# Graph attention, four layers on one core: the adjacency mask turned by DMA engines in place of the tensor engine

## The chip, the cores and the metric

One core of a Trainium2 chip runs the kernel. The metric is the device time of one execution in microseconds (us); a lower one is better. The kernel before took 3196.11 us, the median of 3 runs (3195.84 to 3197.12).

## The reference: what is computed

16 graphs of 1024 nodes with 256 features pass through four layers of graph attention. Each layer normalises the features, cuts them at zero, projects them with a 256 x 256 matrix, and lets each node take a weighted mean over its neighbours. The weights of a row come from one number of the row's node and one of the neighbour, and are zero where the adjacency is zero.

```python
# one layer, cut to what matters; adj is (16, 1024, 1024) int32, here 0 or 1
h  = relu(layernorm(x))
Wh = h @ W
e  = leaky_relu((Wh @ a1)[:, :, None] + (Wh @ a2)[:, None, :])
e  = where(adj == 0, -1e9, e)
x  = x + softmax(e, -1) @ Wh
```

Layers 1 and 2 have another activation and an ELU behind the sum; layer 3 has four heads of 64 features, a bias, a ReLU with the projection added, and a normalisation per head.

## The kernel before, in words

**Tiling.** A graph is called a batch `b`. Its 1024 nodes lie as 8 blocks of 128 on the 128 partitions (`NI = 8`, `P = 128`). `x_b` holds the features, `mask` the adjacency turned over, one byte for each pair: partition and block name the neighbour `j`, the free position names the node `i`. `mask` and `x_b` have three buffers each.

**Loading (`load`, L96 to L124).** `load(b)` is a generator that gives control back at each `yield`. It issues the DMA of the features on the SP queue (L99), and for each block of 128 rows a DMA on the POOL queue that reads int32 and writes bf16 (L106, two ahead, three buffers). For each block, ScalarE sums the squares of adjacency minus a half into `squares` (L117; this later checks that every entry is 0 or 1), TensorE turns the eight 128 x 128 squares of the block into PSUM (L122, tile `misc`), and ScalarE copies them as bytes into `mask` (L123).

**A layer (`attend`, L352).** `weigh` (L268) lays one number of each node along the free axis (L276, on TensorE), and VectorE makes the weights of one neighbour block: maximum or minimum of two terms, times the mask (L280). TensorE multiplies the weights with the projected features (`product`, L367; L471 for the heads of layer 3). `finish` adds the result to `x_b` (L296 to L307, the last addition on POOL), and `project` (L233) makes the projection of the next layer, whose statistics need VectorE and a power on POOL (L227), whose transposes and products run on TensorE (L252, L259), and whose evictions run on ScalarE (L254, L320, L322, L341).

**Order of the work.** Two streams, the even and the odd batches, are traced in turns by hand-written costs (`yield 0.9` and so on), the second `LAG = 120` behind the first; so one stream's last layer lies beside the other's middle layers. The framework then orders each engine's instructions by this priority and by when it takes their inputs to be ready; each engine works through its own queue in that order. `batch(b)` makes `coming = load(b + 2)` and advances it once after each of the eight half-heads of layer 3 (L482), and to its end after the last (L498). `stream(1)` runs `load(1)` ahead of its first batch (L511). `load(0)` and `prepare()`, which fetches and extends the weights, are begun before the streams (L516) and finished behind the first projection (L415), before the first `attend`.

**Output.** After layer 3, POOL does the last scaling and addition (`rescale`, L445, L446), and two DMAs on the SP queue write the batch (L502).

Of the kernel before, what the change touches and what calls it, by code (L numbers as in the profile page):

```python
# [32 lines left out]
F32 = mybir.dt.float32  # L33
BF = mybir.dt.bfloat16
U8 = mybir.dt.uint8
I16 = mybir.dt.int16
I32 = mybir.dt.int32
AF = mybir.ActivationFunctionType
ALU = mybir.AluOpType
AX = mybir.AxisListType  # L40

P = 128
# [17 lines left out]
def short_path(ctx: ExitStack, tc: tile.TileContext, ins: dict, out: bass.AP, bad: bass.AP):  # L60

    nc = tc.nc
    x, adj = ins["x"], ins["adj"]
    B, N, D = x.shape
    H, T, E = ins["L3_a_src"].shape
    NI = N // P
    NK = D // P
    HALF = 512
    NH = N // HALF
    NG = HALF // P  # L70
    EXT = [3, 3, 3, 3 * H]
    AHEAD = 2
    LAG = 120.0

    const = ctx.enter_context(tc.tile_pool(name="const", bufs=1))
    nodes = ctx.enter_context(tc.tile_pool(name="nodes", bufs=3))
    adjs = ctx.enter_context(tc.tile_pool(name="adjs", bufs=3))
    wide = ctx.enter_context(tc.tile_pool(name="wide", bufs=2))
    psum = ctx.enter_context(tc.tile_pool(name="psum", bufs=2, space=bass.MemoryType.PSUM))

    ident = const.tile([P, P], F32, name="ident")
    make_identity(nc, ident)
    ident_b = const.tile([P, P], BF, name="ident_b")
    nc.vector.tensor_copy(ident_b, ident)
    minus_half = const.tile([P, 1], F32, name="minus_half")
    nc.vector.memset(minus_half, -0.5)
    ones = const.tile([P, P], F32, name="ones")
# [2 lines left out]
    squares = const.tile([P, B, NI], F32, name="squares")  # L90
    inverses = const.tile([P, B, NI], F32, name="inverses")


    xs, masks = {}, {}

    def load(b: int):  # L96

        xs[b] = nodes.tile([P, NI, D], F32, name="x_b")
        nc.sync.dma_start(xs[b], x[b].rearrange("(i p) f -> p i f", p=P))  # L99
        mask = masks[b] = nodes.tile([P, NI, N], U8, name="mask")  # L100
        fetched = {}

        def fetch(i: int):

            fetched[i] = adjs.tile([P, N], BF, name="adj_i")
            nc.gpsimd.dma_start(fetched[i], adj[b, ts(i, P), :])  # L106

        for i in range(AHEAD):
            fetch(i)
        yield  # L110
        for i in range(NI):
            if i + AHEAD < NI:
                fetch(i + AHEAD)
            adj_i = fetched.pop(i)

            every = wide.tile([P, N], BF, name="wide")
            nc.scalar.activation(  # L117
                every, adj_i, AF.Square, bias=minus_half, accum_out=squares[:, b, i : i + 1]
            )
            turned = psum.tile([P, NI, P], BF, name="misc")  # L120
            for j in range(NI):
                nc.tensor.transpose(turned[:, j, :], adj_i[:, ts(j, P)], ident_b)  # L122
            nc.scalar.copy(mask[:, :, ts(i, P)], turned)  # L123
            yield  # L124

    edges = ctx.enter_context(tc.tile_pool(name="edges", bufs=NI))
# [8 lines left out]
    bias = const.tile([P, D], F32, name="bias")  # L135
# [132 lines left out]
    def weigh(b: int, column, c, op, into: list):  # L268


        while row_taken:
            yield 0.25
        row_taken.append(b)
        r = psum.tile([P, N], F32, name="row", bufs=1)
        for i in range(NI):
            nc.tensor.transpose(r[:, ts(i, P)], column(i).to_broadcast([P, P]), ident)  # L276
        yield 0.5
        for j in range(NI):
            w = edges.tile([P, N], F32, name=f"weights{b % 2}")
            nc.vector.scalar_tensor_tensor(w, r, c(j), masks[b][:, j, :], op0=op, op1=ALU.mult)  # L280
            into.append(w)
            if j == NI - 1:
                row_taken.pop()
            yield 0.5
# [24 lines left out]
    def batch(b: int):  # L309
        xb = xs.pop(b)  # L310
        if b == 0:
            next(preparing)
        coming = load(b + 2) if b + 2 < B else iter(())

        def begin(l: int):

            V = nodes.tile([P, NI, H, E + 1], F32, name="V", bufs=4).rearrange("p i h e -> p i (h e)")

            def evict(i: int, projected: bass.AP, rstd: bass.AP):
                nc.scalar.activation(V[:, i, D : D + 3], projected[:, D:], AF.Exp, scale=rstd)  # L320
                if l == 2:
                    nc.scalar.mul(V[:, i, :D], projected[:, :D], rstd)  # L322
                else:
                    nc.vector.tensor_scalar(  # L324
                        V[:, i, :D], projected[:, :D], rstd, V[:, i, D : D + 1],
                        op0=ALU.mult, op1=ALU.mult,
                    )

            return V, evict

# [3 lines left out]
        def begin3():  # L334
            h3 = last["h3"] = single.tile([P, NI, D], F32, name="h3")
            V3 = nodes.tile([P, NI, H, E + 1], F32, name="V", bufs=4)
            ex = last["ex"] = small.tile([P, NI, 3 * H], F32, name="ex", bufs=2)

            def evict3(i: int, projected: bass.AP, rstd: bass.AP):
# [3 lines left out]
                nc.gpsimd.tensor_mul(  # L343
                    V3[:, i, :, :E], h3[:, i, :].rearrange("p (h e) -> p h e", h=H),
                    q.to_broadcast([P, H, E]),
                )
                nc.gpsimd.tensor_copy(V3[:, i, :, E:], q)
                nc.gpsimd.tensor_add(xb[:, i, :], xb[:, i, :], beta)

            return V3, evict3  # L350

        def attend(l: int, V: bass.AP, finish, then: int):  # L352

            weights = []
            behind = weigh(
                b, lambda i: V[:, i, D + 2 : D + 3], lambda j: V[:, j, D + 1 : D + 2],
                ALU.min if l == 1 else ALU.max, weights,
            )
            yield from start(behind, b)
            following = begin(then) if then < 3 else begin3()  # L360
            steps = iter(())
            accs = {}

            def product(i: int, j: int):
                if j == 0:
                    accs[i] = accumulator(b)[:, : D + 1]
                nc.tensor.matmul(  # L367
                    accs[i], weights[j][:, ts(i, P)], V[:, j, : D + 1],
                    start=(j == 0), stop=(j == NI - 1),
                )  # L370


            for j in range(NI):
                next(behind)
                product(0, j)
                product(1, j)
                yield 0.9
            for _ in behind:
                pass
            for i in range(NI):  # L380
                if i > 1:
                    for j in range(NI):
                        product(i, j)
                acc = accs.pop(i)
                finish(i, acc)
                if i != 0:
                    yield 3.6
                if i % 2 == 1:

                    yield from steps  # L390
                    steps = project(b, then, xb, i // 2, following[1])
                yield from islice(steps, 1)
            yield 1.0
            yield from steps
            return following[0]
# [16 lines left out]
        for steps in pairs:  # L412
            yield from steps
        if b == 0:
            for _ in chain(loading, preparing):  # L415
                pass
        V = yield from attend(0, V, finish0, 1)
        V = yield from attend(1, V, finish, 2)
        V3 = yield from attend(2, V, finish, 3)


        h3, ex = last["h3"], last["ex"]
        y = single.tile([P, NI, H, E], F32, name="y")
        normed = []
        shape = [P, NI, E]

        def center(h: int):

            yh = y[:, :, h, :]
            head = ts(h, E)  # L430
            nc.gpsimd.tensor_add(yh, yh, bias[:, head].unsqueeze(1).to_broadcast(shape))  # L431
            nc.vector.scalar_tensor_tensor(yh, yh, 0.0, h3[:, :, head], op0=ALU.max, op1=ALU.add)
            mean = small.tile([P, NI], F32, name="mean")
            nc.vector.tensor_reduce(mean, yh, AX.X, ALU.add)
            nc.vector.tensor_scalar_mul(mean, mean, 1.0 / E)
            nc.vector.tensor_sub(yh, yh, mean.unsqueeze(2).to_broadcast(shape))
            square = wide.tile(shape, F32, name="wide")
            nc.scalar.activation(square, yh, AF.Square)
            var = small.tile([P, NI], F32, name="var")
            nc.vector.tensor_reduce(var, square, AX.X, ALU.add)  # L440
            return yh, head, inverse_root(var, NI, L3_EPS, 1.0 / E)
# [18 lines left out]
        for n in range(H * NH):  # L460
            h, g = divmod(n, NH)
# [37 lines left out]
            pass  # L499
        rescale(*normed.pop())  # L500
        for g in range(NH):
            nc.sync.dma_start(  # L502
                out[b, ts(g, HALF), :].rearrange("(i p) f -> p i f", p=P),
                y[:, ts(g, NG)].rearrange("p i h e -> p i (h e)"),
            )
        yield 1.0

# [6 lines left out]
            yield from batch(b)  # L514

    loading, preparing = load(0), prepare()  # L516
    next(loading)
    next(preparing)
    streams = [[0.0, stream(0)], [LAG, stream(1)]]
    while streams:  # L520
        ahead = min(streams, key=lambda s: s[0])
        t = next(ahead[1], None)
# [381 lines left out]
```

## Time and profile before

| What | Value |
|---|---|
| Median of 3 runs | 3196.11 us |
| The profiled execution's own time | 3197.01 us |
| Its span in the profile | 3195.3 us |
| TensorE's mean granted clock | 0.991 |
| ScalarE, busy | 855.3 us (27%) |
| L123, mask eviction on ScalarE | 128 x, mean 1011 ns |
| L117, squares on ScalarE | 128 x, mean 1142 ns |
| L106, adjacency DMA, its issue on POOL | 128 x, mean 605 ns; 3.8 us to landing |
| L99, feature DMA | 16 x 1024 KB, 7.6 us to landing |
| L502, output DMA | 32 x 512 KB, 3.9 us to landing |

The profile gives, for each engine, the time in which it was busy, and for each group of instructions its count, its mean duration, and the idle time of the engine just before it with what ended that. "PE" is TensorE's matmul, "PEld" its weight load, which overlaps it; "DVE" is VectorE, "ACT" ScalarE, "POOL" GpSimd. Matmuls are pipelined: the mean duration of one is longer than the distance from one to the next, so what one costs in a dense row is read from starts in the timeline and not from its duration. The windows view gives busy time for each stretch of time; the timeline lists instructions of one engine with the idle time before them in brackets.

### The profile page before, as it was taken

How to read it: one execution, taken by the hardware profiler on the slowest of the kernel's cores; microseconds unless marked ns; L12 is line 12 of the kernel's file. 1: busy time of each engine (PE TensorE's matmuls, PEld its weight loads, DVE VectorE, ACT ScalarE, POOL GpSimd, SP SyncE). 2: the span in 40 equal slices, each digit the busy share in tenths (PEclk: the TensorE clock that was granted, in tenths of full speed). 3: DMA queues.
4: the chain of work that ended last, by engine and by line, in shares of the span. 5: the costliest groups of instructions: out<-in, count | busy, mean ns of one | idle time of the engine just before them, and what ended most of it. 6: DMA issues, size and time to landing. Idle time of an engine off the chain costs nothing.

```text
span 3195.3 us, 37581 instructions
## 1 busy us (share of the span) xinstructions
PE 3058.6 (96%) x13702; PEld 2112.1 (66%) x13702; DVE 2370.9 (74%) x5244; ACT 855.3 (27%) x1857; POOL 1002.4 (31%) x1286
## 2 busy tenths in 40 slices
PE   7899999999999999999999999999999999999987
PEld 5666776667666686666867667676676767766552
DVE  5576778777787767787687876878768787677756
ACT  3322223222232312323123231232313222232120
POOL 1223324232242322423224232342323323233332
PEclk8999999999999999999999999999999999999998
DMA  4101101111010100101001010111101111000000
GB/s 107 24 7 17 34 4 21 34 20 30 7 37 18 28 19 11 44 11 43 1 14 40 14 40 1 17 37 17 37 1 20 34 17 37 4 14 14 1 14 14
DMA packets 55951, 72.09 MB, mean 23 GB/s; under 512 B 5072, under 2 KB 38992, under 8 KB 55760
## 3 DMA queue, kind: packets, MB, share of 16 engines
q0 software_dynamic: 18432, 33.56, 6.9%
q1 hardware_dynamic: 37328, 36.05, 3.5%
q8 instruction: 111, 1.82, 0.2%
q14 instruction: 80, 0.66, 0.1%
HBM read 86.38 MB, written 16.78 MB: 32 GB/s over the span
## 4 chain that ended last, share of the span: by engine, by line
PE 71%; DVE 17%; POOL 6%; ACT 2%; issue 2%; DMA 1%; ACTq 0%; POOLq 0%; SPq 0%; DVEq 0%
PE acc L367 32%; PE acc L471 21%; PE acc L259 12%; DVE weights L280 8%; PE misc L252 2%; PE row L276 2%; POOL rstd L227 2%; POOL y L431 1%; POOL x_b L307 1%; PE misc L122 1%; DVE centered L244 1%; DVE stats L239 1%; DVE above L305 1%; ACT below L303 1%; PE misc L486 1%
## 5 line engine op out<-in xcount | busy, mean ns | idle before, releaser
L367 PE MATMUL acc<-V,weights 128*128 128x257 f32 x6144 | 1449.8, 384 | 41.9 <-DVE weights L280 20.3
L367 PEld LDWEIGHTS acc<-V,weights 128*128 128x128 f32 x6144 | 1143.8, 191 | 352.3 <-DVE weights L280 99.4
L471 PE MATMUL acc<-weights,V 128*65 128x512 f32 x2048 | 960.6, 593 | 1.9 <-DVE weights L280 1.7
L280 DVE SCALAR_TENSOR_TENSOR weights<-row,ex,mask 128x1024 f32<-128x1024 f32 x512 | 626.9, 1275 | 18.7 <-PE row L276 11.3
L259 PE MATMUL acc<-W,hT 128*128 128x259 f32 (+1 forms) x2048 | 521.7, 392 | 38.0 <-ACT hT L254 22.8
L471 PEld LDWEIGHTS acc<-weights,V 128*65 128x65 f32 x2048 | 272.4, 138 | 354.3 <-issue 311.5
L227 POOL TENSOR_TENSOR rstd<-rstd,minus_half 128x2 f32<-128x2 f32 (+1 forms) x320 | 301.0, 943 | 645.6 <-DVE rstd L226 632.0
L280 DVE SCALAR_TENSOR_TENSOR weights<-row,V,mask 128x1024 f32<-128x1024 f32 x384 | 474.5, 1275 | 33.4 <-PE row L276 32.9
L259 PEld LDWEIGHTS acc<-W,hT 128*128 128x128 f32 x2048 | 378.4, 191 | 170.7 <-ACT hT L254 60.0
L307 POOL TENSOR_TENSOR x_b<-x_b,above 128x256 f32<-128x256 f32 x256 | 191.1, 751 | 813.6 <-DVE above L306 731.1
L303 ACT ACTIVATE below<-acc,inv 128x256 f32<-128x256 f32 x256 | 120.3, 474 | 756.3 <-DVE inv L296 553.4
L239 DVE BATCH_NORM_STATS2 stats<-x_b 128x6 f32<-128x256 f32 x512 | 209.3, 416 | 127.6 <-POOL x_b L307 119.5
L254 ACT COPY hT<-misc 128x512 f32<-128x512 f32 x256 | 147.4, 587 | 372.9 <-PE misc L252 372.8
L244 DVE TENSOR_SCALAR centered<-x_b,mv 128x256 f32<-128x256 f32 x512 | 208.6, 411 | 5.2
L324 DVE TENSOR_SCALAR V<-acc,rstd,V 128x256 f32<-128x256 f32 x256 | 135.2, 537 | 74.6 <-ACT V L320 73.6
L106 POOL DMA_DIRECT2D adj_i<-in_adj_dram x128 | 77.4, 605 | 356.9 <-PE misc L122 115.3
L320 ACT ACTIVATE V<-acc,rstd 128x3 f32<-128x3 f32 x384 | 98.9, 262 | 333.8 <-PE acc L259 333.2
L305 DVE TENSOR_SCALAR above<-acc,inv 128x256 f32<-128x256 f32 x256 | 122.0, 482 | 80.5 <-ACT below L303 77.5
L252 PEld LDWEIGHTS misc<-ident,centered 128*128 128x128 f32 x1024 | 124.1, 141 | 77.5 <-issue 41.1
L252 PE MATMUL misc<-ident,centered 128*128 128x128 f32 x1024 | 158.7, 276 | 15.6 <-DVE rstd L226 8.3
L481 ACT COPY sums<-acc 65x512 f32<-65x512 f32 x128 | 74.3, 581 | 346.4 <-PE acc L471 346.1
L123 ACT CAST mask<-misc 128x1024 uint8<-128x1024 bf16 x128 | 129.1, 1011 | 96.4 <-PE misc L122 96.4
(69 smaller groups left out, 2104.9 us busy)
## 6 DMA issues: line engine op xcount, KB each, us to landing
adj_i<-in_adj_dram POOLq DMA_DIRECT2D x128, 256.0 KB, 3.8
x_b<-in_x_dram SPq DMA_DIRECT2D x16, 1024.0 KB, 7.6
out_dram<-y SPq DMA_DIRECT2D x32, 512.0 KB, 3.9
W<-in_L_gnn_W_dram SPq DMA_DIRECT2D x3, 256.0 KB, 8.9
weights<-in_L_gnn_a_dram SPq DMA_DIRECT2D x3, 256.0 KB, 9.0
W<-in_L_gnn_W_dram SPq DMA_DIRECT2D x2, 128.0 KB, 9.3
weights<-in_L_gnn_a_src_dram SPq DMA_DIRECT2D x1, 128.0 KB, 9.2
weights<-in_L_gnn_a_dst_dram SPq DMA_DIRECT2D x1, 128.0 KB, 7.2
```

Source lines behind the costliest of these rows:

```text
L227: nc.gpsimd.tensor_tensor(r, r, minus_half.to_broadcast([P, n]), op=ALU.pow)
L239: nc.vector.bn_stats(stats, xb[:, 2 * pair + n, :])
L244: nc.vector.tensor_scalar(centered[:, n, :], xb[:, 2 * pair + n, :], mv[:, n, 0:1], 0.0, op0=ALU.subtract, op1=ALU.max,)
L252: nc.tensor.transpose(turned[:, k, ts(n, P)], centered[:, n, ts(k, P)], ident)
L254: nc.scalar.copy(hT, turned)
L259: nc.tensor.matmul(projected, hT[:, k, ts(n, P)], W[l][:, k, :], start=(k == 0), stop=(k == NK - 1),)
L280: nc.vector.scalar_tensor_tensor(w, r, c(j), masks[b][:, j, :], op0=op, op1=ALU.mult)
L303: nc.scalar.activation(below, acc[:, :D], AF.Exp, scale=inv)
L305: nc.vector.tensor_scalar(above, acc[:, :D], inv, 0.0, op0=ALU.mult, op1=ALU.max)
L307: nc.gpsimd.tensor_add(xi, xi, above)
L367: nc.tensor.matmul(accs[i], weights[j][:, ts(i, P)], V[:, j, : D + 1], start=(j == 0), stop=(j == NI - 1),)
L471: nc.tensor.matmul(accT, V3[:, j, h, :], weights[h * NI + j][:, ts(g, HALF)], start=(j == 0), stop=(j == NI - 1),)
```

## The change

The transposes on TensorE and their eviction go. In their place:

- Two scratch matrices in DRAM (`narrows`, one for even and one for odd batches) of 1024 x 1024 bytes. Four DMAs for each batch, on the POOL queue, read 256 rows of int32 each and write them as bytes, rows in the order even, odd of each 256.
- Four DMA transposes for each batch, on the SP queue. Each takes a column strip of the scratch matrix as 1024 rows x 128 two-byte elements and writes it turned, 128 partitions x 1024 two-byte elements, into `mask`. A two-byte element holds a node's pair of neighbours, an even and an odd one, so VectorE's mask operand at L280 becomes every second byte (`masks[b][:, j // 2, :, j % 2]`).
- So that blocks agree, features and output are read and written with partition `p` of block pair `c` holding nodes `256c + 2p` and `256c + 2p + 1` (`in_blocks`).
- ScalarE's squares now read int32 that a plain DMA on SP brings (two buffers), and write in place.
- Outputs are issued by POOL in place of SP.
- Order: `load` has two yields ahead of its eight blocks: behind the casts, and behind features and transposes. `coming` is advanced once more, before layer 2's `attend(2, ...)`; at the start `load(0)` is advanced twice, and `preparing` is finished before `loading`. `keep_in_program_order` holds a cast, or an adjacency DMA, behind what was traced before it on its engine.

```diff
-    adjs = ctx.enter_context(tc.tile_pool(name="adjs", bufs=3))
+    adjs = ctx.enter_context(tc.tile_pool(name="adjs", bufs=2))
...
+    def in_blocks(a: bass.AP) -> bass.AP:
+        return a.rearrange("(c p t) f -> p c t f", p=P, t=2)
...
+    narrows = [dram.tile([N, N // 2], BF, name=f"narrow{n}") for n in range(2)]
     def load(b: int):
+        narrow = narrows[b % 2]
+        rows = narrow.bitcast(U8).rearrange("(c t q) j -> c q t j", t=2, q=P)
+        for c in range(NI // 2):
+            cast = nc.gpsimd.dma_start(
+                rows[c], adj[b, ts(c, 2 * P), :].rearrange("(q t) j -> q t j", t=2)
+            )
+            tc.keep_in_program_order(cast)
+        yield
         xs[b] = nodes.tile([P, NI, D], F32, name="x_b")
...
-            nc.gpsimd.dma_start(fetched[i], adj[b, ts(i, P), :])
...
+        nc.sync.dma_start(xs[b].rearrange("p (c t) f -> p c t f", t=2), in_blocks(x[b]))
+        mask = masks[b] = nodes.tile([P, NI // 2, N, 2], U8, name="mask")
+        for c in range(NI // 2):
+            nc.sync.dma_start_transpose(
+                mask[:, c].rearrange("p n t -> p (n t)").bitcast(BF), narrow[:, ts(c, P)]
+            )
         yield
         for i in range(NI):
...
-            every = wide.tile([P, N], BF, name="wide")
+            adj_i = adjs.tile([P, N], I32, name="adj_i")
+            tc.keep_in_program_order(nc.sync.dma_start(adj_i, adj[b, ts(i, P), :]))
             nc.scalar.activation(
-                every, adj_i, AF.Square, bias=minus_half, accum_out=squares[:, b, i : i + 1]
-            )
-            turned = psum.tile([P, NI, P], BF, name="misc")
-            for j in range(NI):
-                nc.tensor.transpose(turned[:, j, :], adj_i[:, ts(j, P)], ident_b)
-            nc.scalar.copy(mask[:, :, ts(i, P)], turned)
+                adj_i.bitcast(F32), adj_i, AF.Square, bias=minus_half, accum_out=squares[:, b, i : i + 1]
+            )
             yield
...
-            nc.vector.scalar_tensor_tensor(w, r, c(j), masks[b][:, j, :], op0=op, op1=ALU.mult)
+            nc.vector.scalar_tensor_tensor(w, r, c(j), masks[b][:, j // 2, :, j % 2], op0=op, op1=ALU.mult)
...
-            for _ in chain(loading, preparing):
+            for _ in chain(preparing, loading):
...
         V = yield from attend(1, V, finish, 2)
+        next(coming, None)
         V3 = yield from attend(2, V, finish, 3)
...
-            square = wide.tile(shape, F32, name="wide")
+            square = wide.tile(shape, F32, name="wide", bufs=1)
...
-            nc.sync.dma_start(
-                out[b, ts(g, HALF), :].rearrange("(i p) f -> p i f", p=P),
-                y[:, ts(g, NG)].rearrange("p i h e -> p i (h e)"),
+            nc.gpsimd.dma_start(
+                in_blocks(out[b, ts(g, HALF), :]),
+                y[:, ts(g, NG)].rearrange("p (c t) h e -> p c t (h e)", t=2),
             )
...
     loading, preparing = load(0), prepare()
+    next(loading)
     next(loading)
     next(preparing)
```

More of the change, by code (lines that the diff above doesn't have):

```diff
@@ L71, in short_path @@
     EXT = [3, 3, 3, 3 * H]
-    AHEAD = 2
     LAG = 120.0
@@ L76, in short_path @@
     nodes = ctx.enter_context(tc.tile_pool(name="nodes", bufs=3))
-    adjs = ctx.enter_context(tc.tile_pool(name="adjs", bufs=3))
+    adjs = ctx.enter_context(tc.tile_pool(name="adjs", bufs=2))
     wide = ctx.enter_context(tc.tile_pool(name="wide", bufs=2))
     psum = ctx.enter_context(tc.tile_pool(name="psum", bufs=2, space=bass.MemoryType.PSUM))
+    dram = ctx.enter_context(tc.tile_pool(name="dram", bufs=1, space=bass.MemoryType.DRAM))
     ident = const.tile([P, P], F32, name="ident")
     make_identity(nc, ident)
-    ident_b = const.tile([P, P], BF, name="ident_b")
-    nc.vector.tensor_copy(ident_b, ident)
     minus_half = const.tile([P, 1], F32, name="minus_half")
@@ L91, in short_path @@
     inverses = const.tile([P, B, NI], F32, name="inverses")
+    def in_blocks(a: bass.AP) -> bass.AP:
+        return a.rearrange("(c p t) f -> p c t f", p=P, t=2)
     xs, masks = {}, {}
+    narrows = [dram.tile([N, N // 2], BF, name=f"narrow{n}") for n in range(2)]
     def load(b: int):
-        xs[b] = nodes.tile([P, NI, D], F32, name="x_b")
[L99 to L105, printed above, removed]
-            nc.gpsimd.dma_start(fetched[i], adj[b, ts(i, P), :])
-        for i in range(AHEAD):
-            fetch(i)
+        narrow = narrows[b % 2]
[6 more added lines that the diff above has]
+        yield
+        xs[b] = nodes.tile([P, NI, D], F32, name="x_b")
+        nc.sync.dma_start(xs[b].rearrange("p (c t) f -> p c t f", t=2), in_blocks(x[b]))
[4 more added lines that the diff above has]
+            )
         yield
         for i in range(NI):
-            if i + AHEAD < NI:
-                fetch(i + AHEAD)
-            adj_i = fetched.pop(i)
-            every = wide.tile([P, N], BF, name="wide")
+            adj_i = adjs.tile([P, N], I32, name="adj_i")
+            tc.keep_in_program_order(nc.sync.dma_start(adj_i, adj[b, ts(i, P), :]))
             nc.scalar.activation(
-                every, adj_i, AF.Square, bias=minus_half, accum_out=squares[:, b, i : i + 1]
+                adj_i.bitcast(F32), adj_i, AF.Square, bias=minus_half, accum_out=squares[:, b, i : i + 1]
             )
-            turned = psum.tile([P, NI, P], BF, name="misc")
-            for j in range(NI):
-                nc.tensor.transpose(turned[:, j, :], adj_i[:, ts(j, P)], ident_b)
-            nc.scalar.copy(mask[:, :, ts(i, P)], turned)
             yield
```

## The prediction

> **What bounds the kernel now.** I read the page's busy shares first, then the groups, to see whether the engine that loses work is the one that sets the time.
>
> ```profile
> PE 3058.6 (96%) x13702; PEld 2112.1 (66%) x13702; DVE 2370.9 (74%) x5244; ACT 855.3 (27%) x1857; POOL 1002.4 (31%) x1286
> ...
> L280 DVE SCALAR_TENSOR_TENSOR weights<-row,ex,mask 128x1024 f32<-128x1024 f32 x512 | 626.9, 1275 | 18.7 <-PE row L276 11.3
> ...
> L123 ACT CAST mask<-misc 128x1024 uint8<-128x1024 bf16 x128 | 129.1, 1011 | 96.4 <-PE misc L122 96.4
> ```
>
> TensorE is busy 96% of the span; the next, VectorE, 74%. The groups give L122, the transposes, as 84.2 us busy. The windows of a middle stretch say where the change's stage lies:
>
> ```profile
> 1500.00:1520.00 20.00, 17.15 (x83) 12.85 (x82) 14.90 (x32) 6.48 (x19) 4.70 (x6) 1.00 0.42 118
> 1600.00:1720.00 120.00, 117.59 (x526) 74.52 (x525) 97.40 (x203) 37.62 (x72) 42.00 (x49) 1.00 0.10 16
> ```
>
> Columns: stretch, length, then busy time of PE, PEld, DVE, ACT, POOL, granted clock, DMA share, GB/s. In 1600 to 1720, where one stream's last layer carries the 64 transposes of a load, PE is busy 98%, so PE work taken out there should come out of the time. In 1500 to 1520, where one stream changes batch, PE lacks 2.9 us: there other engines' latency decides. The DMA engines are nearly idle (0.10).
>
> What a block of transposes costs PE is read from starts in the timeline:
>
> ```profile
> 1637.28 0.61 PE L122 MATMUL misc<-ident_b,adj_i 128*128 128x128 bf16 x8
> 1637.73 0.41 PE L486 MATMUL misc<-ident,sums 65*128 65x65 f32 x4
> ```
>
> From the first of eight to the next work is 0.45 us, not 0.61 (the last one's end overlaps).
>
> [...] The trace before holds no DMA transpose[...]. [...] The trace shows only the step of one, at 1275 ns.
>
> **The change part by part**, against the profiled execution (3197.01 us; span 3195.3 and 1.7 around it; the median of the runs is 0.9 lower).
>
> *PE's transposes go.* Batches 2 to 15: 14 x 8 blocks x 0.45 = 50 us. A block gives its 0.45 only where PE has other work ready. Of the eight in 1614 to 1714 the last two (1710.95 and 1713.29) are soon followed by PE waits of 0.16 and 0.88 us, so their time would go into those waits. I take 6 of 8: -38 us. Batch 1 the same way, 8 x 0.45 x 0.75: -3. Bounds: 0 and -54.
>
> *ScalarE's evictions go:* 128 x 1.01 = 129 us of an engine at 27%. PE's and PEld's waits for them are 1.1 and 9.4 us; the weight load overlaps, so -1, with -10 as the other end. The squares stay: int32 to f32 is not in the trace, the bf16 row is 1142 ns, and I take the same; half as much again would cost 128 x 0.57 = 73 us of ScalarE, which its idle 73% covers. One `wide` buffer instead of two touches the square of L438 alone, 64 times, with heads some 30 us apart: 0.
>
> *POOL.* Eight issues of 605 ns for each batch (4.8 us) go, and with them the waits for a buffer ahead of them (357 us in all in the groups), in which POOL's queue stood. Added are four casts and two outputs of 256 rows. An issue not shown costs between 605 ns (per instruction) and 1.14 us (256+16 packets against the 144 of 18432/128): 3.6 to 6.8 us for each batch. The casts stand behind layer 1's end, ahead of layer 2, where POOL has room:
>
> ```profile
> 1506.74 1.43 POOL L227 TENSOR_TENSOR rstd<-rstd,minus_half 128x2 f32<-128x2 f32 x2 [1.84 <-DVE rstd L226]
> 1527.45 1.53 POOL L307 TENSOR_TENSOR x_b<-x_b,above 128x256 f32<-128x256 f32 x2 [19.29 <-DVE above L306]
> ```
>
> A 19.29 us gap takes 2.4 to 4.6 us of casts: 0. Without that gap they would hold back a `rstd` or `x_b` for 4.6 us, 14 x 4.6 = 64. The outputs stand behind L446, and queued behind them is the next L307, which DVE's statistics and so PE's next projection wait for. At 1502.62 L307 comes 1.55 us later and hides most; at 1727.4 it comes 0.4 us later, and 0.8 to 1.9 us would show, at a batch change where PE does wait. Over 16 batches, half of them so: +6 to +15, less what the old fetches cost POOL there (0.6 us each, four at these changes). I take +3, bounds -10 and +15.
>
> *DMA engines.* Casting reads what the old fetches read: 6.9% of 3195 us = 220 us, 1.72 us for each 512 KB; a batch's 4 MB is 13.8 us, some 16 with 2 us to land. The plain second read is priced by q1: 36.05 MB in 3.5% (112 us), so 67 MB in 208 us. [...] none of it is waited for if it starts early enough.
>
> *Does it?* The casts come at about 1512. The first square waits for an adjacency DMA that stands on SP behind the features and the four transposes. In program order that square follows the second half-head:
>
> ```profile
> 1613.30 0.58 ACT L481 COPY sums<-acc 65x512 f32<-65x512 f32 x1 [9.18 <-PE acc L471]
> ```
>
> So there are 101 us for casts (16), four transposes and one adjacency DMA (about 4). [...] Later adjacency DMAs have two half-heads, some 25 us, for 512 KB. The mask itself is needed near 1739, later still. SP's other work is only feature loads and these, so its waits stop nobody else.
>
> *DVE's mask read at step two:* 0[...].
>
> *Start.* Now the first weights come at 39.08, after PE waits for adjacency (2.32, 0.49, 0.40, 1.63, 1.76 us) between its transposes; projection 0 ends at 25. After: casts land near 16 + 2, or 30 if the other loads share the engines evenly (DMA share 0.85 in the first 40 us)[...]. I take 36: -3, bounds -14 and +20[...]. Batch 1's squares stand only a few us behind its casts in the trace order, a stall of up to 20 us once, if they aren't put off: +5. *End:* POOL issues the last outputs about 1 us later: +1.
>
> Sum: -38 - 3 - 1 + 3 - 3 + 5 + 1 = -36; 3197 - 36 = 3161. Since the removed POOL waits are priced at nothing and the start may give more, I keep this as it stands.
>
> **Rivals.** *Full gain:* every block's 0.45 us comes out (-54), the masks' waits too (-10), the start gives 10: 3197 - 74 = 3123. For it: PE at 98% to 100% where the blocks lie. Against: 2.9 us lacking at each batch change. *Nothing measurable:* POOL's issues at batch changes (+15) and a late start (+20) eat it: 3161 + 12 + 23 = 3196. For it: POOL's `rstd` is on 2% of the chain. Against: POOL sheds as much as it takes on. *Slower:* ScalarE blocks on the first adjacency DMA behind slow transposes on SP. It decides from (101 - 16 - 4)/4 = 20 us a transpose; every microsecond above costs 4 us for each of 14 batches, since ScalarE works in order and the `hT` and `sums` copies behind the square feed PE. At 23 us: 12 x 14 = 168, 3161 + 168 = 3329. [...] *That it doesn't do what it says* would show as transposes left on PE; none is left in the diff.
>
> **How the numbers follow.** Forecast (3138 to 3188) 0.50; full gain (3110 to 3138) 0.20; nothing measurable (3190 to 3202) 0.08; slower, mostly above 3202, 0.22. What this measurement can tell from no change is about 0.2%, 6.4 us. Faster 0.70, same 0.08, slower 0.22. The range leaves out what lies below 3115 (0.05) and the slow case above 3215 (0.15).
>
> **What would show it.** L122 and L123 gone; PE busy some 50 to 80 us less; L280 still near 1275 ns;[...] ScalarE's wait for `adj_i` DMA small after 200 us; POOL's gap near layer 2's start holding four casts; first L280 at 30 to 40 us. A long ScalarE wait on `adj_i`, or L280 well above 1275 ns, makes the prediction wrong.

## The result, and the profile after

The changed kernel takes 3347.16 us (median of 4, 3345.93 to 3348.35) against 3196.61 us (median of 4) for the kernel before: a ratio of 1.0471, 95% interval 1.0453 to 1.0489. It is 4.7% slower, where 3161 us was forecast and the range ended at 3215. The profiled execution took 3348.35 us, its span is 3346.6 us, and TensorE's mean granted clock is 0.961 instead of 0.991.

From the page of the changed kernel: the busy shares (part 1), then two groups (part 5), which are the mask multiplication on VectorE and the squares on ScalarE.

```profile
PE 3043.0 (91%) x12678; PEld 2089.7 (62%) x12678; DVE 2359.1 (70%) x5243; ACT 742.9 (22%) x1729; POOL 998.5 (30%) x1254
...
L283 DVE SCALAR_TENSOR_TENSOR weights<-row,ex,mask 128x1024 f32<-128x1024 f32 x512 | 626.7, 1274 | 14.0 <-PE row L279 10.8
...
L124 ACT ACTIVATE adj_i<-adj_i,minus_half 128x1024 f32<-128x1024 int32 x128 | 146.8, 1147 | 351.7 <-DMA adj_i<-in_adj_dram 351.3
```

The 1024 transposes are gone from PE (13702 to 12678 instructions), yet PE's busy time fell by only 15.6 us, and its idle time (span less busy) rose from 136.7 to 303.6 us: 166.9 - 15.6 = 151.3 us, which is the whole difference between the spans. VectorE's step of two costs nothing (1274 against 1275 ns). A square costs what it did (1147 against 1142 ns). What is new is the end of the last line: ScalarE, whose queue also holds the copies that feed PE, stood 351 us before the squares. The same in the view of the waits (in total, times, longest), with what PE then waits for:

```profile
ACT adj_i L124 <- DMA adj_i<-in_adj_dram: 351.3, 91, 19.3
...
PE acc L370 <- DVE above L308: 92.3, 17, 16.3
...
PE misc L490 <- ACT sums L485: 39.3, 14, 6.1
```

The same two waits of PE in the kernel before were short:

```profile
PE acc L367 <- DVE above L305: 7.7, 17, 1.2
...
PE misc L486 <- ACT sums L481: 6.9, 8, 0.9
```

PE's wait for `hT` grew as well, from 22.8 to 45.3 us, but its longest is 13.6 us at the start, and it stays when the squares are moved (e1).

The transfers themselves (page, part 6: count, KB each, median us from issue to landing):

```profile
adj_i<-in_adj_dram SPq DMA_DIRECT2D x128, 512.0 KB, 4.2
...
narrow<-in_adj_dram POOLq DMA_DIRECT2D x64, 256.0 KB, 9.8
out_dram<-y POOLq DMA_DIRECT2D x32, 512.0 KB, 7.5
mask<-narrow SPq DMA_TRANSPOSE x64, 3.8
```

An adjacency load came in at about what was forecast (4 us), and a transpose landed in 3.8 us; an output takes 7.5 us where it took 3.9, but the view of the waits puts no engine's wait down to its end. So no slow transfer explains the loss. The timeline at one change of batch shows what happens (start, duration, engine, line, what; in brackets the idle time before it and what ended it), engine by engine: POOL, SP, ScalarE, PE.

```profile
1579.62 2.74 POOL L106 DMA_DIRECT2D narrow<-in_adj_dram  x4
...
1593.73 5.18 SPq L116 DMA_TRANSPOSE mask<-narrow  x4
1599.02 18.55 SPq L122 DMA_DIRECT2D adj_i<-in_adj_dram  x8
...
1585.85 0.26 ACT L323 ACTIVATE V<-acc,rstd 128x3 f32<-128x3 f32 x1 [0.55 <-PE acc L262]
1603.60 1.15 ACT L124 ACTIVATE adj_i<-adj_i,minus_half 128x1024 f32<-128x1024 int32 x1 [17.49 <-DMA adj_i<-in_adj_dram]
...
1608.53 1.15 ACT L124 ACTIVATE adj_i<-adj_i,minus_half 128x1024 f32<-128x1024 int32 x1 [2.43 <-DMA adj_i<-in_adj_dram]
...
1609.67 0.82 ACT L306 ACTIVATE below<-acc,inv 128x256 f32<-128x256 f32 x2
...
1598.11 1.13 PE L370 MATMUL acc<-V,weights 128*128 128x257 f32 x4 [1.38 <-DVE weights L283]
1610.79 10.83 PE L370 MATMUL acc<-V,weights 128*128 128x257 f32 x40 [11.55 <-DVE above L308]
```

Read it downwards. The casts are issued at 1579.62; SP issues the transposes 14.1 us later and the first adjacency load at 1599.02, and its square starts at 1603.60: 24 us after the casts. ScalarE had nothing ahead of that square after 1586.1 and stood 17.49 us. Behind the square on its queue is `below` (L306), which VectorE's `above` (L308) needs, and PE waits 11.55 us for that. All eight squares of the load follow within 19 us, where I had put the first of them some 100 us behind the casts.

PE pays twice. The windows view over the same stretch (stretch, length, busy us of PE, PEld, DVE, ACT, POOL with counts, granted clock, DMA share, GB/s):

```profile
1603.00:1610.00 7.00, 0.00 (x0) 0.00 (x0) 0.00 (x0) 3.95 (x7) 0.00 (x0) 0.50 0.57 189
1610.00:1614.00 4.00, 3.21 (x8) 2.59 (x9) 3.84 (x6) 2.39 (x5) 1.51 (x2) 0.50 0.65 196
1614.00:1618.00 4.00, 4.00 (x19) 3.45 (x18) 4.00 (x7) 1.82 (x4) 0.00 (x0) 0.91 0.65 203
1618.00:1622.00 4.00, 4.00 (x22) 3.52 (x21) 3.12 (x9) 2.22 (x3) 2.16 (x3) 1.00 0.45 131
```

In the 4 us after the stop PE gets through 8 matmuls at half clock, busy for 3.21 us of them; later it does 22 in as long. That is why its busy time fell by so much less than its instructions.

### The profile page after: what moved, and what is told of

It is laid out like the page before. It is cut to its first block, busy times and chain, and to the rows that moved or that the text cites. A ratio compares the mean times of both kernels' runs of the same rounds, so it can differ in the third digit from the quotient of the medians.

```text
span 3346.6 us, 35757 instructions
## 1 busy us (share of the span) xinstructions
PE 3043.0 (91%) x12678; PEld 2089.7 (62%) x12678; DVE 2359.1 (70%) x5243; ACT 742.9 (22%) x1729; POOL 998.5 (30%) x1254
## 3 DMA queue, kind: packets, MB, share of 16 engines
q1 hardware_dynamic: 98256, 103.17, 11.3%
## 4 chain that ended last, share of the span: by engine, by line
PE 63%; DVE 17%; POOL 7%; DMA 5%; ACT 3%; SPq 3%; issue 2%; ACTq 0%; POOLq 0%; DVEq 0%
PE acc L370 29%; PE acc L475 19%; PE acc L262 10%; DVE weights L283 7%; DMA adj_i<-in_adj_dram 4%; PE misc L255 2%; SPq L116 2%; POOL rstd L230 2%; PE row L279 2%; DVE stats L242 2%; POOL y L435 1%; POOL x_b L310 1%; ACT adj_i L124 1%; DVE centered L247 1%; DVE above L308 1%
## 5 line engine op out<-in xcount | busy, mean ns | idle before, releaser
L370 PE MATMUL acc<-V,weights 128*128 128x257 f32 x6144 | 1468.1, 388 | 120.3 <-DVE above L308 92.3
L370 PEld LDWEIGHTS acc<-V,weights 128*128 128x128 f32 x6144 | 1164.4, 193 | 451.6 <-issue 176.5
L283 DVE SCALAR_TENSOR_TENSOR weights<-row,ex,mask 128x1024 f32<-128x1024 f32 x512 | 626.7, 1274 | 14.0 <-PE row L279 10.8
L262 PE MATMUL acc<-W,hT 128*128 128x259 f32 (+1 forms) x2048 | 538.0, 403 | 83.3 <-ACT hT L257 45.3
L262 PEld LDWEIGHTS acc<-W,hT 128*128 128x128 f32 x2048 | 393.3, 198 | 220.2 <-ACT hT L257 105.6
L283 DVE SCALAR_TENSOR_TENSOR weights<-row,V,mask 128x1024 f32<-128x1024 f32 x384 | 474.5, 1274 | 49.6 <-PE row L279 49.6
L306 ACT ACTIVATE below<-acc,inv 128x256 f32<-128x256 f32 x256 | 119.5, 472 | 753.4 <-DVE inv L299 527.9
L308 DVE TENSOR_SCALAR above<-acc,inv 128x256 f32<-128x256 f32 x256 | 121.3, 479 | 192.1 <-ACT below L306 191.4
L124 ACT ACTIVATE adj_i<-adj_i,minus_half 128x1024 f32<-128x1024 int32 x128 | 146.8, 1147 | 351.7 <-DMA adj_i<-in_adj_dram 351.3
L247 DVE TENSOR_SCALAR centered<-x_b,mv 128x256 f32<-128x256 f32 x512 | 198.8, 391 | 4.4
L435 POOL TENSOR_TENSOR y<-y,bias 128x512 f32<-128x512 f32 x64 | 81.7, 1277 | 370.3 <-DVE y L493 343.5
```

Of the source, the lines that this page charges most:

```text
L124: nc.scalar.activation(adj_i.bitcast(F32), adj_i, AF.Square, bias=minus_half, accum_out=squares[:, b, i : i + 1])
L247: nc.vector.tensor_scalar(centered[:, n, :], xb[:, 2 * pair + n, :], mv[:, n, 0:1], 0.0, op0=ALU.subtract, op1=ALU.max,)
L262: nc.tensor.matmul(projected, hT[:, k, ts(n, P)], W[l][:, k, :], start=(k == 0), stop=(k == NK - 1),)
L283: nc.vector.scalar_tensor_tensor(w, r, c(j), masks[b][:, j // 2, :, j % 2], op0=op, op1=ALU.mult)
L308: nc.vector.tensor_scalar(above, acc[:, :D], inv, 0.0, op0=ALU.mult, op1=ALU.max)
L370: nc.tensor.matmul(accs[i], weights[j][:, ts(i, P)], V[:, j, : D + 1], start=(j == 0), stop=(j == NI - 1),)
```

## The experiments

Ratios are to the kernel before, with 95% intervals. "Period" is the distance between the feature loads of one stream's successive batches in the middle of the run, read from SP's timeline, so the time of two batches: 387.1 us before, 407.3 us after. Single distances within one kernel differ by up to 3 us (379.2 to 382.3 in e6), so a difference of half a microsecond between periods says nothing.

**e1_squares_held.** The square may no longer be moved ahead of what was traced before it on ScalarE. Nothing else is edited: the same instructions, the same transfers. The loads do spread out with the squares, since each waits for a buffer that a square gives free: four are issued in 106.64 us at the batch change below, where the changed kernel issues eight in 18.55.

```diff
-            nc.scalar.activation(
+            tc.keep_in_program_order(nc.scalar.activation(
                 adj_i.bitcast(F32), adj_i, AF.Square, bias=minus_half, accum_out=squares[:, b, i : i + 1]
-            )
+            ))
```

> The changed kernel, with each square on ScalarE held behind what was traced before it on ScalarE, so that it follows the half-head of layer 3 it was written behind, not the casts. Nothing else is changed; the DMA traffic is the same. Theory (queue order: ScalarE stands in front of a square whose data has yet to pass casts, transposes and its own load): ScalarE's wait of 351 us for adj_i falls below 30 us, PE's idle time falls from 303 us to about 140, and the time to 3130 to 3165 us. Rival (the added DMA traffic itself, in bursts of 0.9 of the engines, holds the kernel up): 3300 to 3347 us, since the traffic stays.

Measured: 3183.8 us, 0.996 (0.9945 to 0.9974), period 383.9. ScalarE's wait in the view of the waits of this kernel, and the first square of a load with the instruction ahead of it in its timeline, whose casts were issued at 1501.27:

```profile
ACT adj_i L124 <- DMA adj_i<-in_adj_dram: 42.0, 12, 17.6
```

```profile
1606.34 0.58 ACT L485 COPY sums<-acc 65x512 f32<-65x512 f32 x1 [9.18 <-PE acc L475]
1606.82 1.15 ACT L124 ACTIVATE adj_i<-adj_i,minus_half 128x1024 f32<-128x1024 int32 x1
```

The square now stands behind `sums`, 105.6 us after the casts, and waits for nothing; the 42.0 us are all waits of batches 0 and 1. PE's idle time falls from 303.6 to 170.3 us, by 133 us; of these its wait for `above` (ahead of L370) gives 84.6 (92.3 to 7.7) and that for `sums` 34.5 (39.3 to 4.8), while the one for `hT` stays at 44.1. So the loss sat in what stood behind the squares on ScalarE, and the place of the squares in a queue was worth 163 us. The traffic as such is out as the cause, since the same bytes move; loads in a burst, with the squares in their late place, were not tried. The time is still 19 us above the range that I expected, so something else costs some 20 to 50 us.

**e2_no_squares.** No squares and no adjacency loads; the values they leave are set to one. So the check of the entries is left out; the masks are made as in the changed kernel.

```diff
+    nc.vector.memset(squares, 1.0)
...
-            adj_i = adjs.tile([P, N], I32, name="adj_i")
-            tc.keep_in_program_order(nc.sync.dma_start(adj_i, adj[b, ts(i, P), :]))
-            nc.scalar.activation(
-                adj_i.bitcast(F32), adj_i, AF.Square, bias=minus_half, accum_out=squares[:, b, i : i + 1]
-            )
```

> The changed kernel without the squares and without the adjacency loads that feed them: the check that every entry is 0 or 1 is left out. Casts, transposes and outputs on POOL stay. Theory (queue order): 3120 to 3150 us, the same as with squares held or up to 15 us less. Rival (DMA traffic): a third to a half of the added traffic is gone, so a third to a half of the loss, 3270 to 3300 us. Rival (POOL: casts and outputs hold back its other work): 3320 us or more.

Measured: 3150.17 us, 0.9856 (0.984 to 0.9873), period 383.4. Against e1 the period hardly differs (383.9), so in mid-run held squares cost next to nothing. The 34 us between the two, where I had expected 15 at most, lie at the start: the feature load of batch 2, the first behind it, is issued at 343.3 us in e1 and at 314.7 in e2, so 28.6 us are lost by then.

**e3_outputs_on_sp**, **e5_held_outs_sp**, **e6_no_squares_outs_sp.** Outputs issued by SP again, in the changed kernel, in e1 and in e2 (so e6 leaves out what e2 leaves out).

```diff
-            nc.gpsimd.dma_start(
+            nc.sync.dma_start(
                 in_blocks(out[b, ts(g, HALF), :]),
```

> The changed kernel with the outputs issued by SP again, all else as changed. Theory (queue order): no part of the loss comes from there, 3335 to 3360 us. Rival (POOL's two output issues of 0.75 us each at every batch change hold back the additions behind them): 16 x 1.5 = 24 us less, 3323 us, or more if each is felt twice.

> The changed kernel with the squares held in program order and the outputs issued by SP again. Two batches took 387.1 us in the middle of the kernel before and 383.9 with the squares alone held; the 64 us-per-kernel's worth of transposes would allow 387.1 - 16 x 0.45 = 379.9. Theory (the rest of the saving is lost where POOL's two output issues hold back an addition to x_b, at the batch change): 380 us for two batches and 3150 to 3160 us in all. Rival (POOL's issue is hidden, and the outputs cost something only in the kernel as changed): 383.9 and 3180 us or more.

> The changed kernel without squares and their adjacency loads (the check of the entries is left out), outputs issued by SP. What the transposes on TensorE cost before, 128 x 0.45 = 57 us, should then come out in full: theory 3110 to 3125 us, 380 us for two batches. Rival (blocks of transposes filled time in which PE would wait anyway, so that a quarter or more is lost as the prediction had it): 382 us or more for two batches and 3130 us or more.

Measured: e3 3325.98 us, 1.0398 (1.038 to 1.0415); e5 3167.56 us, 0.9913 (0.9896 to 0.9929), period 381.4; e6 3133.33 us, 0.9807 (0.9791 to 0.9823), period 380.4. Three pairs, one answer: outputs on POOL cost 21, 16 and 17 us. For e3 the rival was right, with 3323 us, and what I called theory there was wrong. The timeline of e2 shows where, POOL and then PE:

```profile
1685.70 1.32 POOL L445 TENSOR_TENSOR y<-y,x_b 128x512 f32<-128x512 f32 x1
1687.32 1.53 POOL L501 DMA_DIRECT2D out_dram<-y  x2 [0.30 <-POOL y L445]
1688.87 0.73 POOL L305 TENSOR_TENSOR x_b<-x_b,above 128x256 f32<-128x256 f32 x1
...
1692.05 4.57 PE L257 MATMUL acc<-W,hT 128*128 128x259 f32 x12 [4.22 <-DVE above L303]
```

The same place in the kernel before:

```profile
1726.10 1.26 POOL L446 TENSOR_TENSOR y<-y,x_b 128x512 f32<-128x512 f32 x1
1727.77 0.73 POOL L307 TENSOR_TENSOR x_b<-x_b,above 128x256 f32<-128x256 f32 x1 [0.41 <-DVE above L306]
...
1731.01 2.92 PE L259 MATMUL acc<-W,hT 128*128 128x259 f32 x12 [1.85 <-ACT hT L254]
```

POOL waits 0.30 us for its own last result and issues for 1.53 us; the addition into `x_b` starts 1.85 us after the output's last addition instead of 0.41. PE's wait grows from 1.85 to 4.22 us, and the next 12 matmuls take 4.57 us instead of 2.92. Most of that is not the outputs' doing, for e6, which has them on SP, shows nearly the same at that place:

```profile
1678.81 4.48 PE L257 MATMUL acc<-W,hT 128*128 128x259 f32 x12 [3.48 <-DVE above L303]
```

Outputs account there for 0.74 us of the wait and 0.09 us of the matmuls; why the wait is longer than in the kernel before even without them, no run shows. It is the three pairs that price the outputs, 1.0 to 1.3 us a batch.

e5 and e6 also measure what leaving out the transposes gives. Two batches hold 16 blocks of 0.45 us, 7.2 us (that is 58 us in all, not the 64 of my expectation for e5). The period of e6 is 6.7 us below that of before, but e6 does without the squares as well; in e5, which keeps them, it is 5.7 us below. For the whole run both came in some 8 us above what I expected. So for e6 the period was that of the theory and the total that of its rival.

**e4_loads_on_act.** The adjacency loads go out from ScalarE's queue, so that they no longer stand behind casts and transposes on SP.

```diff
-            tc.keep_in_program_order(nc.sync.dma_start(adj_i, adj[b, ts(i, P), :]))
+            tc.keep_in_program_order(nc.scalar.dma_start(adj_i, adj[b, ts(i, P), :]))
```

> The changed kernel with the int32 adjacency loads issued by ScalarE's own queue, so that they no longer stand behind the transposes, and so behind the casts, on SP. Theory (queue order): a square then waits for its own load alone, about 4 us for the first two of a batch instead of 15 to 19, and some 2 us for each of the others as now; of 351 us of ScalarE's wait about 150 to 200 go, and the time is 3180 to 3270 us. Rival (DMA traffic): 3330 us or more, since the same bytes move.

Measured: 3190.22 us, 0.9982 (0.9973 to 0.999). The time is within what was expected, though only 111 us of ScalarE's wait went and not 150 to 200; but it doesn't separate the two causes it was meant to. The load is held in program order on ScalarE, and the square that reads it can't go ahead of it, so this holds the squares too. What it adds to e1 is the load's flight (3.6 us from issue to landing), now in front of nearly every square: ScalarE waited 239.9 us for `adj_i`, 96 times, at most 15.7. It is 6 us slower than e1, although its start is 7 us shorter (feature load of batch 2 at 336.1 us, in e1 at 343.3), so behind the start the waits go with some 14 us. Spread out beside layer 3, such waits are cheap; in one row they are not.

**e7_casts_later.** The extra advance of `coming` before layer 2 is taken out, so that casts start with layer 3.

```diff
         V = yield from attend(1, V, finish, 2)
-        next(coming, None)
         V3 = yield from attend(2, V, finish, 3)
```

> The changed kernel without the extra advance of the load ahead of layer 2: casts, transposes and squares are written later, the casts after the first half-head of layer 3. Squares are not held. Theory (the framework puts the squares close behind the casts wherever those stand, since it takes their data as landed sooner than it is): the stall moves along, ScalarE still waits over 200 us for adj_i, and the time is 3290 to 3380 us. Rival (the loss comes of the place of the casts, in the batch change): most of it goes, 3150 to 3220 us.

Measured: 3400.63 us, 1.0643 (1.0625 to 1.0661), slower still, and 20 us above what the theory expected; ScalarE waited 389.8 us for `adj_i`. In its timeline the stall has moved along with the casts:

```profile
1678.04 1.44 POOL L106 DMA_DIRECT2D narrow<-in_adj_dram  x2
...
1692.06 5.19 SPq L116 DMA_TRANSPOSE mask<-narrow  x4
1697.34 18.55 SPq L122 DMA_DIRECT2D adj_i<-in_adj_dram  x8
...
1701.95 1.15 ACT L124 ACTIVATE adj_i<-adj_i,minus_half 128x1024 f32<-128x1024 int32 x1 [15.43 <-DMA adj_i<-in_adj_dram]
```

Again the first square starts 24 us behind the casts, and ScalarE stands 15 us for it. So the stall doesn't belong to the change of batch; the squares are put behind the casts wherever those are, and in layer 3 ScalarE's `sums` stand behind them: PE waited 168.0 us for those in all (39.3 in the changed kernel).

**e8_transposes_twice.** Each transpose is issued twice, to make the chain of transfers ahead of the first square longer.

```diff
-        for c in range(NI // 2):
+        for c in list(range(NI // 2)) * 2:
             nc.sync.dma_start_transpose(
```

> The changed kernel with the four DMA transposes of each batch issued twice, to the same place; squares not held. Each takes 1.3 us of SP's queue. Theory (the first square waits for its adjacency load, which stands behind the transposes): 5.2 us more wait for each of 16 batches, 80 us or somewhat more with what PE needs to speed up again: 3410 to 3450 us, unless the squares are ordered later for it. Rival (the casts alone set the wait, or DMA traffic): within 20 us of 3347.

Measured: 3377.98 us, 1.0573 (1.0556 to 1.0591): 31 us more than the changed kernel, where the theory had 63 to 103 and the rival at most 20. From its timeline, ScalarE and PE:

```profile
1602.61 0.26 ACT L323 ACTIVATE V<-acc,rstd 128x3 f32<-128x3 f32 x1 [0.55 <-PE acc L262]
1626.31 1.15 ACT L124 ACTIVATE adj_i<-adj_i,minus_half 128x1024 f32<-128x1024 int32 x1 [23.44 <-DMA adj_i<-in_adj_dram]
1627.46 0.45 ACT L306 ACTIVATE below<-acc,inv 128x256 f32<-128x256 f32 x1
...
1628.58 11.73 PE L370 MATMUL acc<-V,weights 128*128 128x257 f32 x44 [15.09 <-DVE above L308]
```

The wait for the first square did grow by 5.95 us (17.49 to 23.44), about the 5.2 us that the four transposes more take to issue. But the first `below` now stands behind one square; in the changed kernel it stood behind three. From the last short activation ahead of the stall to `below` it is 24.85 us against 23.82. PE's stop grew by 3.5 us. That is one load of two. At the next one the casts were issued at 1774.44, and the first square again starts 29 us behind them:

```profile
1803.42 1.15 ACT L124 ACTIVATE adj_i<-adj_i,minus_half 128x1024 f32<-128x1024 int32 x1 [7.50 <-DMA adj_i<-in_adj_dram]
```

But there ScalarE stands only 7.50 us, where it stood 14.63 at the same load of the changed kernel, because the `wide` and `sums` behind the first square are now ahead of it. In all, ScalarE's wait for `adj_i` is 356.6 us against 351.3. So a longer chain of transfers moves every first square back by its length, but the framework moved other work ahead of about half of them, and the price stayed well below what I expected.

**e9_start_too.** e5, and the squares of batches 0 and 1 spread as well: batch 0's lie beside its layers 0 and 1, and the casts, features and transposes of batch 1 are traced behind batch 0's first layer, ahead of its own start.

```diff
+    def beside(steps, more):
+        while True:
+            try:
+                t = next(steps)
+            except StopIteration as done:
+                return done.value
+            if t > 3:
+                next(more, None)
+            yield t
...
-            for _ in chain(preparing, loading):
+            for _ in preparing:
...
-        V = yield from attend(0, V, finish0, 1)
-        V = yield from attend(1, V, finish, 2)
+        V = yield from beside(attend(0, V, finish0, 1), loading)
+        if b == 0:
+            next(second)
+            next(second)
+        V = yield from beside(attend(1, V, finish, 2), loading)
...
-            for _ in load(first):
+            for _ in second:
...
-    loading, preparing = load(0), prepare()
+    loading, preparing, second = load(0), prepare(), load(1)
```

> The kernel with squares held and outputs on SP, and in addition the start mended: batch 0's squares are spread over layers 0 and 1 of batch 0 in place of standing ahead of them, and batch 1's casts and transposes are written after batch 0's layer 0, ahead of its squares. Two batches should still take 381 us. Theory (what is left of the loss beside the kernel without squares, 3168 against 3133, lies at the start, where PE was busy 57.5 us of 120 to 200 us against 75.3): 3135 to 3152 us. Rival (the squares and their loads cost the 34 us elsewhere, spread over the whole run): 3160 us or more.

Measured: 3152.51 us, 0.986 (0.9844 to 0.9877), period 381.4 as in e5. It is the fastest that computes everything, 1.4% faster than the kernel before. The windows view of 120 to 200 us in e5, e9 and e6 (columns as above; PE busy is the first number after the length):

```profile
120.00:200.00 80.00, 57.51 (x243) 46.00 (x243) 38.18 (x112) 24.35 (x57) 25.70 (x40) 0.83 0.66 119
```

```profile
120.00:200.00 80.00, 69.04 (x296) 55.34 (x295) 50.76 (x134) 26.61 (x62) 26.94 (x43) 0.89 0.39 79
```

```profile
120.00:200.00 80.00, 75.28 (x343) 56.76 (x342) 60.90 (x147) 17.25 (x46) 27.89 (x47) 1.00 0.42 53
```

In e5 PE does 243 matmuls there at a clock of 0.83, in e9 296, in e6 343. The first square of batch 1 stood 17.89 us on ScalarE in e5; it is the 17.6 us of e1 and the 18.04 us of the changed kernel. The start is thus worth 15 us (e5 to e9); the time is half a microsecond above the range that I expected. Most of the 19 us from e9 to e6 still lie there too: the feature load of batch 2 is issued at 332.3 us in e9 and at 314.3 in e6, 18.0 us apart. That speaks against the rival, for which the squares and their loads cost their time all over the run. Which of the two costs it at the start was not separated.

## Why the prediction was wrong, step by step

**The step that failed** is in "Does it?": "In program order that square follows the second half-head", and so "there are 101 us". That is where the square was traced, not where it stood. The framework orders an engine's instructions by when it takes their inputs to be ready, and on ScalarE it put the first square right behind an instruction that ended 6 us after the first cast was issued (1586.11 against 1579.62), while the square's data came 24 us after it. ScalarE then stood 14 to 19 us for the first square of a load in mid-run and up to 2.7 us for later ones. e1 shows it by putting the squares back: 3347 to 3184. e7 shows that they follow the casts. That the framework expects the adjacency loads to land earlier than they do is my inference from e1, e7 and e8; its estimate is in no trace. The trace of before held a hint: there the squares stand in pairs up to 25 us apart (L117 at 1635.95 and 1637.09, at 1661.59 and 1662.72), not one behind each half-head as written.

**The cost of the stall** adds up from PE: 133 us of its idle time and 33 us of its busy time go between the changed kernel and e1, 166 us of span. The busy part goes with the clock, whose mean is 0.961 in the one and 0.981 in the other. I had no term for it.

**PE's transposes**, -41 with batch 1's: right in direction, and near. My factor of 6 blocks in 8 is 5.4 of 7.2 us a pair of batches; 5.7 come out in e5, which keeps the squares, and 6.7 in e6, which does without them, 46 to 54 us over eight pairs. Since single distances differ by up to 3 us, the factor can't be fixed more closely. e6 as a whole is 63 us below before, in the place of the "full gain" rival, but without the squares.

**Transfers** were about as priced where a trace of before priced them: casts 14.1 us (16 said, of it 2 to land: the old fetch's 3.8 us less its 1.72), an adjacency load 4.2 (4 said). A transpose took 3.8 us to landing and 1.3 us of SP; its price was my estimate, since the trace of before holds none. The two queues carry 18.2% of the 16 engines' span. The casts stand in POOL's gap at no visible cost: the four at 1579.62 took 2.74 us, and POOL then waited 29.09 us for `above`.

**VectorE and the squares:** 1274 and 1147 ns, as taken. Both were my estimates: the trace of before shows the mask read at a step of one (1275 ns) and the squares of bf16 (1142 ns), and the changed kernel's trace is the first with the step of two and with int32.

**Outputs on POOL:** +3 taken, 16 to 21 measured, above the upper bound of +15. I had let half of the batches hide them and the old fetches' 0.6 us come back. The period shows 2.5 us for two batches (383.9 to 381.4), more than the 0.8 to 1.9 us of one paying batch in two; which of the two assumptions failed was not separated.

**Start:** the first weights came at 27.85 us, 11 before those of the old kernel, where -3 was taken; the bound of +20 was my estimate, and no trace showed it. The gain was given back: "a stall of up to 20 us once" was 18.04 us on ScalarE, taken at +5, and in 120 to 200 us PE was busy 55.76 us against 71.65 before.

**The rivals.** "Slower" had the right place, ScalarE blocked on the first adjacency load with copies for PE behind it (`sums`, and `below` where it named `hT`), and a near total (3329). Its mechanism was not the one: it needed transposes above 20 us each, and they landed in 3.8. Nor does adding transposes bring what its price of 4 us per load for each microsecond says: 1.3 us more for each of four would be 73 us over 14 loads, and e8 measured 31. "Nothing measurable" had outputs and start as its two costs, and both were real; e1 at 3184 shows what they leave of the gain.

## What to carry to other kernels

A line's place in the source is not its place in an engine's queue: before a wait is called hidden, ask what may be moved in front of it, and look in the trace of before whether such instructions already stand away from where they are written. An instruction that waits for a long chain of transfers, on an engine that also feeds the bound, has to be held in place (163 us here), or at least its waits spread out. Price a stop of PE with the slow clock after it (0.50 for some 4 us after 11.55 us here), and put no issue in front of the addition that the next projection waits for (16 to 21 us here).

## What the runs showed of the hardware

**A stop of PE can cost more than its length.** After 11.55 us in the changed kernel the clock is 0.50 for some 4 us. After 4.22 us in e2 it is 0.50 in the first 2 us and 0.64 in the next 2:

```profile
1692.00:1694.00 2.00, 1.95 (x5) 1.57 (x6) 1.07 (x4) 0.54 (x2) 1.61 (x3) 0.50 1.01 394
1694.00:1696.00 2.00, 2.00 (x7) 1.62 (x6) 0.87 (x3) 0.51 (x2) 0.76 (x2) 0.64 0.65 266
```

There the 12 matmuls take 4.57 us instead of 2.92; after 1.85 us in the kernel before the clock stays at 1.00. Between these, the traces of the two kernels show it at 1.00 after stops of 2.34 us (changed kernel, at 349.99) and 2.61 us (before, at 341.46). After 2.70 us in the changed kernel (at 1986.12) it is 0.66 in the first 2 us and 0.50 in the next 2, and after 3.04 us in the kernel before (at 2492.84) 0.79 and then 0.50. What decides it is not shown. Over the changed kernel I estimate some 41 us: PE was busy 3043.0 us there and 3002.3 us in e6 with the same 12678 instructions.

**The DMA transpose is cheap here:** 256 KB, two bytes an element, DRAM to SBUF, 3.8 us from issue to landing and 1.29 us of SP's queue each (four in 5.18 us).

**Here order outweighed traffic.** The DMA queues q0 and q1 carried 137 MB in the changed kernel, and about as large a share of the engines' time in e1 (7.2% and 12.0% against 6.9% and 11.3%), with 163 us between the two times.
